# A pair-product kernel with batch normalisation: another order on GpSimd, and another cutting of the stores

## Chip, cores, metric

The kernel runs on one core of a Trainium2 chip. The metric is device time in microseconds. The profile is of one execution, and its span is about 1.7 us shorter than the timed figure of the same execution.

## The reference, cut

```python
# r_xi, r_xj: (1024, 39, 16); W: (1, 16, 16); gamma, beta: (741,)
rows, cols = np.tril_indices(39, k=-1)                   # 741 pairs (row, col), col < row
cross = xj[:, rows, :, None] * xi[:, cols, None, :]      # (1024, 741, 16, 16)
mean, var = ...                                          # of each pair, over (0, 2, 3)
normed = (cross - mean) * rsqrt(var + 1e-5) * gamma + beta
out = normed[:, :, None] * W                             # (1024, 1, 741, 16, 16), float32
```

The output has 777 MB, the inputs 6 MB. Row r has r pairs, "columns" below; one column of one sample is 256 floats in each of 128 partitions, 128 KB.

## The kernel before

Each partition holds 8 samples, worked on two at a time. A tile is one row for two samples. Row r and row 38-r share one half of a large buffer `y_sb`, and the two halves alternate. "Set" means such a pair of rows: 38 columns, two samples, 9.96 MB. The statistics, some 45 us at the start, are left out here.

```python
def products(n):                       # y = xj * (scaled xi): ScalarE 24 instructions a tile, GpSimd 8
    xs = xs_of.pop(n)
    for t in range(T):                 # T = 2 samples, sample 0 first
        for i in range(E):
            product(n, nc.scalar if i < E - POOL_I else nc.gpsimd, t, i, xs[:, t])

def store(n, c0, c1):
    r, t0, _ = tiles[n]
    n0 = first[r]
    nc.sync.dma_start(
        out_v[:, t0 : t0 + T, (n0 + c0) * EE : (n0 + c1) * EE],
        view(n)[:, :, c0:c1, :].rearrange("p t n e -> p t (n e)"),
    )

def bounds(r):                         # PIECE = 14
    pieces = -(-r // PIECE)
    return tuple(q * r // pieces for q in range(pieces + 1))

def finish(n):                         # y = (y + t) * w
    ...                                # GpSimd: the last 13% of the columns
    for c0, c1 in zip(bounds(r), bounds(r)[1:]):
        for c in range(c0, min(c1, split)):
            stt(...)                   # VectorE: one instruction a column, both samples
        store(n, c0, c1)

for n in range(1, len(tiles)):
    if n + 1 < len(tiles):
        products(n + 1)
    if n + 2 < len(tiles):
        scale_xi(n + 2)                # GpSimd
    if n >= RAW:                       # RAW = 2
        finish(n)
```

## Time and profile before

| | before |
|---|---|
| timed, median of 3 | 1929.05 us |
| span of the profiled run | 1927.5 us |
| VectorE, ScalarE, GpSimd busy | 90%, 86%, 79% |
| stores of the output | 289 |

No engine is busy for the whole span. The row to read is that of the transfers, stage by stage; the prediction shows it. A share of 1.01 is the highest that this profile holds over a whole stretch; it is read here as DMA engines that are never idle, and a lower share as engines that had to wait for pieces.

### The profile page before, as it was taken

What the parts mean: (1) busy time and instruction counts of PE and PEld (TensorE: products, weight loads), DVE (VectorE), ACT (ScalarE), POOL (GpSimd) and SP (SyncE); (2) the same over time, 40 slices, a digit from 0 to 9 for tenths busy, and PEclk for the clock granted to TensorE, in tenths of its full rate; (3) what the DMA queues carried; (4) which work ended last, traced back from release to release, by engine and by line L of the source; (5) the groups of instructions that cost most, each with busy time, mean ns of one, the idle gap of its engine ahead of it and who ended that gap; (6) DMA issues with size and microseconds to landing.
All of it is one profiled execution on the core that took longest, in us unless ns stands there. A gap on an engine that the chain in (4) does not pass through costs nothing. (4 is left out here: it accounts for less than half of the span.)

```text
span 1927.5 us, 10086 instructions
## 1 busy us (share of the span) xinstructions
PE 25.5 (1%) x132; PEld 23.8 (1%) x132; DVE 1732.3 (90%) x2603; ACT 1663.4 (86%) x3690; POOL 1528.2 (79%) x1918
## 2 busy tenths in 40 slices
PE   2200000000000000000000000000000000000000
PEld 2200000000000000000000000000000000000000
DVE  5999999999989899999999999999999999888886
ACT  7999888888888988889888898888888888888752
POOL 6898888887878787979787878888888877777654
DMA  3799999999999999999999999999999999999998
GB/s 125 326 421 421 420 421 421 421 421 421 424 426 423 424 425 423 426 423 426 423 421 421 421 421 416 411 420 416 414 415 414 415 414 415 405 406 402 393 389 373
DMA packets 80174, 783.66 MB, mean 407 GB/s; under 512 B 4800, under 2 KB 5824, under 8 KB 14816
## 3 DMA queue, kind: packets, MB, share of 16 engines
q1 hardware_dynamic: 79328, 779.95, 96.8%
q10 hardware_dynamic: 720, 2.94, 0.4%
q14 instruction: 77, 0.63, 0.1%
q0 software_dynamic: 48, 0.13, 0.1%
q8 instruction: 1, 0.02, 0.0%
HBM read 6.00 MB, written 776.99 MB: 406 GB/s over the span
## 5 line engine op out<-in xcount | busy, mean ns | idle before, releaser
L222 DVE SCALAR_TENSOR_TENSOR y_sb<-y_sb,st_sb,w_dve 128x512 f32<-128x512 f32 x2542 | 1679.7, 742 | 158.5 <-issue 147.1
L130 ACT ACTIVATE y_sb<-xs,xj_sb 128x256 f32<-128x256 f32 (+33 forms) x3600 | 1613.4, 542 | 218.7 <-DMA out_dram<-y_sb 166.2
L132 POOL TENSOR_SCALAR y_sb<-xs,xj_sb 128x256 f32<-128x256 f32 (+33 forms) x1200 | 604.3, 527 | 198.5 <-DMA out_dram<-y_sb 131.3
L214 POOL TENSOR_TENSOR y_sb<-y_sb,w_sb 128x1024 f32<-128x1024 f32 (+4 forms) x138 | 441.8, 3202 | 11.5
L150 POOL TENSOR_TENSOR xs<-xi_sb,st_sb 128x576 f32<-128x576 f32 (+37 forms) x150 | 188.0, 1253 | 146.4 <-ACT y_sb L130 146.4
L210 POOL TENSOR_SCALAR y_sb<-y_sb,st_sb 128x512 f32<-128x512 f32 x384 | 259.6, 693 | 1.7 <-ACT y_sb L130 1.7
L130 ACT ACTIVATE y_sb<-xi_sb,xj_sb 128x304 f32<-128x304 f32 x52 | 23.9, 533 | 0.0
L191 DVE TENSOR_TENSOR y_sb<-y_sb,w_dve 128x5120 f32<-128x5120 f32 (+3 forms) x5 | 20.9, 4205 | 3.2 <-ACT y_sb L181 3.2
L183 POOL TENSOR_SCALAR y_sb<-y_sb,st_sb 128x512 f32<-128x512 f32 x18 | 13.5, 772 | 7.5 <-DVE st_sb L396 7.5
L383 PE MATMUL ps<-y_sb 39*128 39x38 f32 (+37 forms) x76 | 16.9, 398 | 20.1 <-DVE st_sb L390 13.9
L383 PEld LDWEIGHTS ps<-y_sb 39*128 39x128 f32 x76 | 16.4, 328 | 20.7 <-DVE st_sb L390 14.2
L281 DVE TENSOR_REDUCE y_sb<-y_sb 128x78 f32<-128x1248 f32 x8 | 11.6, 1448 | 3.8 <-ACT y_sb L275 3.6
L266 POOL TENSOR_TENSOR y_sb<-xj_sb,y_sb 128x1248 f32<-128x1248 f32 x4 | 9.3, 2321 | 6.3 <-ACT y_sb L319 6.3
L181 ACT ACTIVATE y_sb<-y_sb,st_sb 128x512 f32<-128x512 f32 x20 | 14.2, 798 | 0.0
L260 DVE TENSOR_REDUCE y_sb<-xj_sb 128x78 f32<-128x1248 f32 x4 | 5.8, 1449 | 8.5 <-DMA xj_sb<-in_r_xj_dram 8.5
L275 ACT ACTIVATE y_sb<-y_sb 128x1248 f32<-128x1248 f32 x8 | 9.8, 1228 | 2.2 <-POOL y_sb L266 2.2
L266 POOL TENSOR_TENSOR y_sb<-xi_sb,y_sb 128x1248 f32<-128x1248 f32 x4 | 9.3, 2318 | 0.0
L130 ACT ACT_TABLE_LOAD x1 | 1.3, 1283 | 7.8 <-DMA xi_sb<-in_r_xi_dram 7.8
L298 PE MATMUL ps_g<-y_sb 128*39 128x79 f32 x48 | 7.2, 339 | 18.6 <-DVE y_sb L286 18.6
L298 PEld LDWEIGHTS ps_g<-y_sb 128*39 128x39 f32 x48 | 6.1, 183 | 19.5 <-POOL y_sb L266 11.2
L132 POOL TENSOR_SCALAR y_sb<-xi_sb,xj_sb 128x304 f32<-128x304 f32 x12 | 5.9, 509 | 0.0
L260 DVE TENSOR_REDUCE y_sb<-xi_sb 128x78 f32<-128x1248 f32 x4 | 5.8, 1442 | 0.0
(42 smaller groups left out, 23.3 us busy)
## 6 DMA issues: line engine op xcount, KB each, us to landing
out_dram<-y_sb SPq DMA_DIRECT2D x56, 3072.0 KB, 11.7
out_dram<-y_sb SPq DMA_DIRECT2D x56, 2816.0 KB, 13.7
out_dram<-y_sb SPq DMA_DIRECT2D x52, 2560.0 KB, 14.2
out_dram<-y_sb SPq DMA_DIRECT2D x32, 3328.0 KB, 16.5
out_dram<-y_sb SPq DMA_DIRECT2D x16, 3584.0 KB, 17.8
out_dram<-y_sb SPq DMA_DIRECT2D x23, 2304.0 KB, 15.6
out_dram<-y_sb SPq DMA_DIRECT2D x20, 2048.0 KB, 22.4
out_dram<-y_sb SPq DMA_DIRECT2D x8, 1792.0 KB, 18.9
```

Source lines behind the costliest of these rows:

```text
L130: nc.scalar.activation(y, src, AF.Copy, scale=scale)
L132: engine.tensor_scalar(y, src, scale, 1.0, ALU.mult, ALU.mult)
L150: nc.gpsimd.tensor_tensor(xs, xi_sb[:, t0 : t0 + T, 0:r, :], s_sb[:, :, n0 : n0 + r, :].to_broadcast([P, T, r, E]), ALU.mult,)
L181: nc.scalar.activation(y[:, :, c, :], y[:, :, c, :], AF.Identity, bias=t_c, scale=s_c)
L183: nc.gpsimd.tensor_scalar(y[:, :, c, :], y[:, :, c, :], s_c, t_c, ALU.mult, ALU.add)
L191: nc.vector.tensor_tensor(y[:, :, c0:c1, :], y[:, :, c0:c1, :], w_dve.unsqueeze(1).to_broadcast([P, T, c1 - c0, EE]), ALU.mult,)
L210: nc.gpsimd.tensor_scalar(y[:, :, c, :], y[:, :, c, :], t_sb[:, n0 + c : n0 + c + 1], 1.0, ALU.add, ALU.mult)
L214: nc.gpsimd.tensor_tensor(y[:, :, split:r, :], y[:, :, split:r, :], w_sb.unsqueeze(1).to_broadcast([P, T, r - split, EE]), ALU.mult,)
L222: stt(y[:, :, c, :], y[:, :, c, :], t_sb[:, n0 + c : n0 + c + 1], w_dve.to_broadcast([P, T, EE]), ALU.add, ALU.mult,)
L266: nc.gpsimd.tensor_tensor(devs[n % 7], sources[x][:, t0 : t0 + T], shift[:, x : x + 1, :].unsqueeze(3).to_broadcast([P, T, F, E]), ALU.sub ...
L298: nc.tensor.matmul(acc[0:F, 0 : 2 * F + 1], lhs, fb[:, t], start=t == 0, stop=t == NT - 1)
L383: nc.tensor.matmul(ps_v[:, :, first[r] - n0 : first[r] - n0 + r], pick[:, r, :], stq[:, :, 0:r], start=True, stop=True,)
```

## The change

The intent is to keep the transfers supplied in the late rows. GpSimd adds bias and weight to its own columns before it turns to products that may have to wait for a buffer. Rows over 28 leave in four pieces, the first and the last short, and the last piece in two stores, one for each sample. Rows up to 19 leave whole, except the first tile, whose three pieces stay.

```diff
-PIECE = 14
+WHOLE = 19
+LONG = 28
@@ def store
-        nc.sync.dma_start(
-            out_v[:, t0 : t0 + T, (n0 + c0) * EE : (n0 + c1) * EE],
-            view(n)[:, :, c0:c1, :].rearrange("p t n e -> p t (n e)"),
-        )
+        step = 1 if r > LONG and c1 == r else T
+        for t in range(0, T, step):
+            nc.sync.dma_start(
+                out_v[:, t0 + t : t0 + t + step, (n0 + c0) * EE : (n0 + c1) * EE],
+                view(n)[:, t : t + step, c0:c1, :].rearrange("p t n e -> p t (n e)"),
+            )
@@ def bounds
-        pieces = -(-r // PIECE)
-        return tuple(q * r // pieces for q in range(pieces + 1))
+        if r <= WHOLE:
+            return (0, r)
+        if r <= LONG:
+            return (0, r // 2, r)
+        return (0, r // 5, r // 2, r - r // 5, r)
@@ the loop over tiles
+            if n == 1:
+                products(2)
+                scale_xi(3)
+                continue
+            if n + 2 < len(tiles):
+                scale_xi(n + 2)
+            finish(n)
             if n + 1 < len(tiles):
                 products(n + 1)
-            if n + 2 < len(tiles):
-                scale_xi(n + 2)
-            if n >= RAW:
-                finish(n)
```

## The prediction

> **What bounds the kernel now.** I read the page first, its slices above all: they show which resource is full in which stage.
>
> ```profile
> span 1927.5 us, 10086 instructions
> DMA  3799999999999999999999999999999999999998
> GB/s 125 326 421 421 420 421 421 421 421 421 424 426 423 424 425 423 426 423 426 423 421 421 421 421 416 411 420 416 414 415 414 415 414 415 405 406 402 393 389 373
> ```
>
> From the third slice on, the transfers are full, with three levels of rate: 421, then about 424, then 421 again, and a decline from slice 25. No engine is full in the same sense: VectorE 90%, ScalarE 86%, GpSimd 79%. The table by stretch (columns: time, busy time and count of PE, PEld, DVE, ACT and POOL, granted clock, DMA share, GB/s) says what the levels are:
>
> ```profile
> 335.00:382.00 47.00, 0.00 (x0) 0.00 (x0) 42.68 (x65) 42.36 (x96) 38.95 (x50) 1.00 1.01 421
> ...
> 711.00:758.00 47.00, 0.00 (x0) 0.00 (x0) 42.27 (x65) 41.43 (x94) 34.41 (x47) 1.00 1.01 424
> ...
> 1087.00:1134.00 47.00, 0.00 (x0) 0.00 (x0) 43.63 (x66) 41.72 (x96) 38.79 (x50) 1.00 1.01 422
> ...
> 1557.00:1604.00 47.00, 0.00 (x0) 0.00 (x0) 42.27 (x65) 41.76 (x96) 37.11 (x47) 1.00 0.99 414
> ...
> 1792.00:1839.00 47.00, 0.00 (x0) 0.00 (x0) 40.79 (x63) 34.61 (x54) 33.07 (x29) 1.00 0.94 394
> 1839.00:1886.00 47.00, 0.00 (x0) 0.00 (x0) 41.80 (x65) 27.31 (x40) 27.57 (x29) 1.00 0.91 383
> ```
>
> A "set" below is row r with row 38-r for two samples: always 38 columns, 38 x 256 KB = 9.96 MB. With rows 20 to 23 a set leaves in four transfers (two pieces of each row) at 421.1 GB/s, with rows 24 to 28 in three (the short row is whole) at 424.3, with rows 29 and 30 in four (the long row in three pieces) at 421 again, each time with the share at 1.01. So one more transfer per set costs 9.96/421.1 - 9.96/424.3 = 0.18 us, and the bytes alone take 23.48 - 3 x 0.18 = 22.94 us (434 GB/s). Below a share of 1.01 the transfers starve. Why they do at the end is in the chain of work that ended last (start, us, what):
>
> ```profile
> 1833.23 5.62 POOL y_sb L214
> ...
> 1838.86 9.46 DMA out_dram<-y_sb
> ...
> 1848.60 6.00 POOL y_sb L132 x8
> 1854.60 2.23 POOL xs L150
> 1856.83 3.35 POOL y_sb L210 x5
> ...
> 1860.24 5.60 POOL y_sb L214
> ...
> 1865.86 9.46 DMA out_dram<-y_sb
> ```
>
> This is a ring: the last piece of a tile leaves (9.46), which frees the buffer for GpSimd's products (6.00); behind these in GpSimd's order stand the scaling of xi (2.23) and the finishing of the previous tile's own pairs (3.35 + 5.60), which releases that tile's last piece. It comes to 27.0 us per set of row 38, where three transfers need 23.5. Last, the beginning, in the two-us stretches:
>
> ```profile
> 76.00:78.00 2.00, 0.00 (x0) 0.00 (x0) 2.00 (x4) 2.00 (x6) 2.00 (x5) 1.00 0.99 415
> 78.00:80.00 2.00, 0.00 (x0) 0.00 (x0) 2.00 (x4) 2.00 (x6) 2.00 (x3) 1.00 0.05 19
> 80.00:82.00 2.00, 0.00 (x0) 0.00 (x0) 2.00 (x4) 2.00 (x6) 1.92 (x3) 1.00 0.00 0
> 82.00:84.00 2.00, 0.00 (x0) 0.00 (x0) 2.00 (x4) 2.00 (x6) 2.00 (x3) 1.00 0.61 253
> ```
>
> Here the queue is empty and waits for the third tile's first piece, while VectorE is full. It stays full until about 240: in that time the backlog of transfers is only building up.
>
> **What the Trainium skill says.** "SBUF — State Buffer", section "The DMA setup-cost knee", puts the asymptote at 16 ports x 27.2 GB/s = 436 GB/s; the 434 GB/s found above from the two levels agrees, so the saturated middle has nothing left but the cost of cutting. "DMA: Bandwidth & Descriptors", section "Measured (HBM→SBUF, 128 partitions, SWDGE, issued from GpSimd)", gives about 10.5 ns per packet in tiny loads. Each store here has 256 rows, 16 per DMA engine, and one completion packet: 17 x 10.5 = 0.179 us, close to my 0.18. This trace cannot say whether the price is per packet or per transfer, since all its stores have the same number of rows; the change has stores of 128 rows, and there it matters. The same page, "Rules for kernel authors", wants at least 1 MiB per DMA; the new half pieces of 5 to 7 columns have 0.66 to 0.92 MB, so the direction of that cost is against the change. "GPSIMD Engine Reference", section 3.1, puts a two-input operation near 2.5 cycles an element; the trace's 5.60 us for 2560 elements are 2.19 ns, 2.6 cycles at the page's 1.2 GHz. It agrees, and the finishing cannot be had for less: it can only be moved.
>
> **The change, part by part.**
> 1. *GpSimd finishes first.* The same instructions, in another order. It takes the ring apart: the finishing of tile n no longer stands behind products that wait for a transfer. What remains for row 38 is a ring over two sets: last piece landed, ScalarE's 24 products 16.7 us (24 instructions in 16.73), VectorE's 33 instructions 21.8 us (33 in 21.81), last piece. GpSimd has 2.2 + 9.0 after ScalarE's last product, inside VectorE's 21.8, and so drops out.
> 2. *Rows over 28 in four pieces.* For row 38: 7, 12, 12, 7 columns instead of 12, 13, 13. VectorE does only 2 of the last 7 (GpSimd has five), and the transfer that frees sample 0 is 7 x 128 KB: 2.1 us, plus 1.7 us to land (9.46 for 3.4 MB, less 7.8 at 434 GB/s; an estimate). The ring: 16.7 + 21.8 + 2.1 + 1.7 = 42.3 us for two sets, plus whatever backlog stands ahead of it; two sets of transfers take 47 to 48. So the transfers should be full again in rows 31 to 38, with 5 us to spare in the worst row and more in the others.
> 3. *Its price.* Rows 29 to 38 go from three transfers to five: 40 tiles x 2 = +80. Rows 15 to 19 whole: 16 tiles less one each, and three of the four tiles of row 19: -19. From 289 to 350, +61. Per transfer: 61 x 0.18 = +11.0 us. Per packet: 310 x 16 + 350 data and completion packets per engine instead of 289 x 17, +397 x 10.6 ns = +4.2 us. A full set of rows 29 to 37 would then run at 9.96/(22.94 + 6 x 0.18) = 415 GB/s, or about 418 per packet. That is what rows 31 to 35 have now, starved: there the change wins nothing or little; rows 29 and 30 lose.
> 4. *Row 19 whole.* The third tile's first piece now leaves after 9 VectorE instructions (0.66 us each), the whole tile after 17. The queue is empty then, so it stays empty 8 x 0.66 = 5.3 us longer, and as everything behind it is full, this shifts all. The second tile whole leaves 5 us later too, but both its halves are out before 88 either way. I add nothing for rows 15 to 18.
>
> The sum. Before: first bytes at 50.2; transfers 78 sets x 22.94 + 289 x 0.18 = 1841.3; idle from 50 to 84, from the shares of the stretches, 8.8; end of the last bytes to end of span 2.0 (stretches of the end). Left over: 1927.5 - 1902.3 = 25.2 us of starving, nearly all after 1180 (the rates of the 47-us stretches from 1181 against 421 give 20 up to 1886, and the tail the rest). After: 50.2 + 1789.3 + (56 to 63 of cutting, middle 60) + 8.8 + 5.3 + 2.0 + remaining starving. For that last term I take 5 us: 0.5 us a set in row 38, where the ring with its backlog is nearly as long as two sets, somewhat less in 36 and 37, and a residue. Sum 1920.6 us of span; the timed figure stands 1.5 over the span, so **1922 us**, a gain of 0.4%. In short: +20 from the ring, -8 from cutting, -5 from the start.
>
> **Rivals.**
> - *The price is per transfer.* Then 1925; per packet, 1919. For packets speaks the 17 x 10.5; for transfers, that each has its own completion. The rates of rows 29 to 37 will tell: 415 or 418.
> - *GpSimd becomes the late one elsewhere.* Its products of n+1 now come after the finishing of n, so VectorE could wait at the start of n+1 for GpSimd instead of ScalarE. Then the transfers would starve in the middle, and with the price of cutting the time would be about 1940 to 1945. Against it: in row 38 GpSimd needs 2.2 + 9.0 + 6.0 = 17 us after ScalarE's last product, and VectorE is busy on tile n for 21.8 of them; with rows 27 and 11, GpSimd's 12 us stand beside 15 us of VectorE. The order gives GpSimd no work more.
> - *The early backlog is too thin for whole rows.* Until 240 VectorE is full at 21.8 us a set against 23.5 of transfer. By hand: whole row 19 leaves at 87 and runs to 99, the next leaves at 98; row 20's pieces at 105 and 110 and whole row 18 at 120 meet a queue busy to 111, 117 and 123. It holds, with half a us to spare at one place; if not, 3 to 8 us more: 1925 to 1930.
> - *Much faster.* Even with all starving and all cutting gone, 50.2 + 1789.3 + 14.1 + 2.0 = 1856 would be the end; with the cutting that this profile prices, 1912 to 1919. A gain of 2% (1890.5) is out of reach unless cutting is free.
>
> **Range and chances.** Low end 1911: price per packet and no starving left make 1913.5, two less for what I round. High end 1936: price per transfer, half the starving stays and the start costs more. All of it lies within 2% (1890.5 to 1967.6). Faster 0.01, same 0.97, slower 0.02 (a new wait in the middle that I don't see).
>
> **What would show it.** Step 1: no GpSimd products or finishing in the chain at the end, and the DMA share after 1650 back at 1.00 to 1.01. Step 3: 415 to 418 GB/s in rows 29 to 37 at full share (now 421 in rows 29 and 30), 424 in rows 20 to 23 (now 421). Step 4: the queue empty from 83 to 88 instead of 78 to 83. Wrong would be: VectorE waiting for GpSimd's products in the middle, a share under 1.00 between 90 and 1180, or rows 29 and 30 still at 421, which would make cutting cheaper than I think.

## The result

The changed kernel takes 1924.28 us (median of 6, 1924.05 to 1924.9) against 1929.10 for the kernel before on the same chip: ratio 0.9976, interval 0.9963 to 0.9989. That is a gain of 0.24%, which at a threshold of 2% is "same".

The slices of the profile after:

```profile
span 1923.2 us, 10490 instructions
...
DMA  3699999999999999999999999999999999999999
GB/s 125 273 425 423 425 425 424 424 425 425 424 425 423 424 425 426 423 424 424 423 418 419 417 418 418 418 417 416 411 412 413 415 412 412 412 410 412 412 412 391
```

The decline at the end has nearly gone, but from row 29 on the level before it is lower. The same stretches as were shown of before:

```profile
335.00:382.00 47.00, 0.00 (x0) 0.00 (x0) 41.43 (x64) 39.99 (x91) 36.40 (x51) 1.00 1.01 425
1087.00:1134.00 47.00, 0.00 (x0) 0.00 (x0) 42.56 (x66) 41.33 (x95) 39.15 (x50) 1.00 1.01 418
1557.00:1604.00 47.00, 0.00 (x0) 0.00 (x0) 42.44 (x65) 42.35 (x96) 37.42 (x49) 1.00 1.00 413
1792.00:1839.00 47.00, 0.00 (x0) 0.00 (x0) 42.30 (x65) 36.76 (x65) 37.47 (x39) 1.00 0.99 409
1839.00:1886.00 47.00, 0.00 (x0) 0.00 (x0) 43.63 (x66) 31.03 (x46) 32.17 (x29) 1.00 0.99 412
```

Against before: rows 20 to 23 gain (421 to 425 in the first line), rows 29 and 30 lose at a full share (422 to 418 in the second), row 35 is about the same (414 and 413), and the last rows gain (394 and 383 to 409 and 412). The chain of work at the end:

```profile
1837.27 9.70 DMA out_dram<-y_sb
...
1847.08 2.14 ACT y_sb L132 x3
...
1849.87 4.48 ACT y_sb L132 x7
1854.35 6.59 DVE y_sb L230 x10
...
1860.99 10.63 DMA out_dram<-y_sb
```

GpSimd has left the chain. In its place is transfer, ScalarE's products, VectorE, transfer. The beginning, in two-us stretches:

```profile
66.00:68.00 2.00, 2.00 (x10) 2.00 (x10) 2.00 (x1) 2.00 (x6) 0.00 (x0) 1.00 0.07 31
68.00:70.00 2.00, 0.13 (x1) 0.00 (x1) 2.00 (x1) 2.00 (x6) 0.00 (x0) 1.00 0.00 0
70.00:72.00 2.00, 0.67 (x3) 0.67 (x4) 1.97 (x3) 0.71 (x2) 0.80 (x1) 1.00 0.36 150
...
82.00:84.00 2.00, 0.00 (x0) 0.00 (x0) 2.00 (x4) 2.00 (x6) 0.00 (x0) 1.00 0.46 195
84.00:86.00 2.00, 0.00 (x0) 0.00 (x0) 2.00 (x4) 2.00 (x6) 1.81 (x2) 1.00 0.00 0
86.00:88.00 2.00, 0.00 (x0) 0.00 (x0) 2.00 (x4) 2.00 (x5) 1.92 (x3) 1.00 0.00 0
88.00:90.00 2.00, 0.00 (x0) 0.00 (x0) 2.00 (x4) 2.00 (x6) 2.00 (x3) 1.00 0.75 315
```

The queue is empty from 83 to 88.5, where before it was empty from 78 to 83. That stretch is about as long as before, only later. The additional 5 us of idle time lie at 66 to 71, before the second tile, which is whole too; the kernel before has shares of 0.89 to 1.06 there.

### The profile page after: what moved, and what is told of

Read it like the earlier page. It is cut to its first block, busy times and chain, and to the rows that moved or that the text cites. A ratio compares the mean times of both kernels' runs of the same rounds, so it can differ in the third digit from the quotient of the medians.

```text
span 1923.2 us, 10490 instructions
## 1 busy us (share of the span) xinstructions
PE 25.5 (1%) x132; PEld 23.8 (1%) x132; DVE 1733.6 (90%) x2602; ACT 1663.9 (87%) x3690; POOL 1534.1 (80%) x1918
## 5 line engine op out<-in xcount | busy, mean ns | idle before, releaser
L196 DVE TENSOR_TENSOR y_sb<-y_sb,w_dve 128x1536 f32<-128x1536 f32 (+3 forms) x4 | 20.9, 5219 | 3.2 <-ACT y_sb L186 3.2
L391 PE MATMUL ps<-y_sb 39*128 39x38 f32 (+37 forms) x76 | 16.9, 398 | 20.1 <-DVE st_sb L398 13.9
L391 PEld LDWEIGHTS ps<-y_sb 39*128 39x128 f32 x76 | 16.4, 328 | 20.7 <-DVE st_sb L398 14.2
L289 DVE TENSOR_REDUCE y_sb<-y_sb 128x78 f32<-128x1248 f32 x8 | 11.6, 1448 | 3.5 <-ACT y_sb L283 3.3
L186 ACT ACTIVATE y_sb<-y_sb,st_sb 128x512 f32<-128x512 f32 x20 | 14.2, 800 | 0.0
L306 PEld LDWEIGHTS ps_g<-y_sb 128*39 128x39 f32 x48 | 6.1, 183 | 19.5 <-POOL y_sb L274 11.2
```

Of the source, the lines that this page charges most:

```text
L186: nc.scalar.activation(y[:, :, c, :], y[:, :, c, :], AF.Identity, bias=t_c, scale=s_c)
L196: nc.vector.tensor_tensor(y[:, :, c0:c1, :], y[:, :, c0:c1, :], w_dve.unsqueeze(1).to_broadcast([P, T, c1 - c0, EE]), ALU.mult,)
L306: nc.tensor.matmul(acc[0:F, 0 : 2 * F + 1], lhs, fb[:, t], start=t == 0, stop=t == NT - 1)
L391: nc.tensor.matmul(ps_v[:, :, first[r] - n0 : first[r] - n0 + r], pick[:, r, :], stq[:, :, 0:r], start=True, stop=True,)
```

## The experiments

All were correct, and all were timed over five rounds (four or five runs of each) beside the kernel before, whose median was between 1929.2 and 1929.6 us. Four calls were made: the first four runs, the next three, the four after those, and the last. Runs of one call shared a chip. The theory at the start is the prediction's: GpSimd's order breaks the ring that starves the late rows, and the cutting and the whole row 19 mostly cost. The rival is that the pieces break it and the order does nothing.

### 1. The order alone

```diff
 (kernel before, the loop over tiles alone)
-            if n + 1 < len(tiles):
-                products(n + 1)
+            if n == 1:
+                products(2); scale_xi(3)
+                continue
             if n + 2 < len(tiles):
                 scale_xi(n + 2)
-            if n >= RAW:
-                finish(n)
+            finish(n)
+            if n + 1 < len(tiles):
+                products(n + 1)
```

> The kernel before with only GpSimd's order changed (289 stores as before). Theory 1 (the order breaks the ring, the cutting and the whole row 19 only cost): no starving ring is left, so 50.2 + 1841.3 of transfers + 8.8 idle at the start + 2.0 + 5 to 8 of starving (the last piece of 13 columns makes the two-set ring 16.7 + 21.8 + 7.8 + 1.7 = 48.0 us against 47, so rows 36 to 38 stay a little short) = 1907 to 1910 of span, 1909 to 1912 us timed, that is 12 to 15 us under the whole change. Rival (the short last pieces break the ring, the order does nothing): 1929 us as before, with GpSimd's products and finishing still in the chain at the end.

It took 1927.15 us (ratio 0.9989, 0.9975 to 1.0002). The theory falls: 12 to 15 us less than the whole change were expected, and it was 3 us more. GpSimd did leave the chain, as it should, and the time hardly moved. The timeline of ScalarE in row 38 shows why (start, duration, what, idle before it and what ended that):

```profile
1821.73 16.73 ACT L130 ACTIVATE y_sb<-xs,xj_sb 128x608 f32<-128x608 f32 x24 [7.26 <-DMA out_dram<-y_sb]
1849.37 16.72 ACT L130 ACTIVATE y_sb<-xs,xj_sb 128x608 f32<-128x608 f32 x24 [10.91 <-DMA out_dram<-y_sb]
1872.66 16.73 ACT L130 ACTIVATE y_sb<-xs,xj_sb 128x608 f32<-128x608 f32 x24 [6.58 <-DMA out_dram<-y_sb]
```

From the first start to the third are two sets: 50.9 us, or 25.5 for each. In the kernel before the same three starts are at 1821.50, 1848.50 and 1875.42, 27.0 for each. So a second ring, ScalarE to VectorE to the last piece, was nearly as long as the GpSimd ring. The chain of this run has the last piece landing 11.6 to 12.8 us after its issue in this stage, not 9.5. The likely reason is the piece before it, still in the queue: it has 13 columns, 7.8 us of transfer at 434 GB/s, and was issued 8 VectorE instructions (5.3 us) earlier. An estimate: the 2.5 us left, 7.8 of its own and 1.7 to land make 12.0.

### 2. The pieces alone

```diff
 (whole change, that edit of the loop undone)
-            finish(n)
             if n + 1 < len(tiles):
                 products(n + 1)
+            if n + 2 < len(tiles):
+                scale_xi(n + 2)
+            if n >= RAW:
+                finish(n)
```

> The whole change, but GpSimd's old order. Theory 1: the ring stays, shorter by its last piece: products 6.0 + scaling 2.2 + finishing 9.0 + last piece 4.2 and 1.7 to land = 23.1 us and whatever stands ahead of it in the queue, against 23.8 of transfers in row 38; with the cost of cutting (+4) and the start (+5) between 1928 and 1938 us. Rival (the pieces alone break the ring): 1924 us, like the whole change.

It took 1925.03 us (ratio 0.9977), beside 0.9976 for the whole change. In time the rival holds: within the whole change the order adds nothing that can be measured. GpSimd did not leave this chain, though. It stands in it from 1847 to 1887, with 24.6 us between its starts (1847.03 and 1871.66), and the ScalarE ring has 24.7 (1822.15 to 1871.58 for two sets). With the new pieces the two rings are equally long, so taking one away gains nothing.

### 3. Without the halves

```diff
-        step = 1 if r > LONG and c1 == r else T
+        step = T
```

> The whole change, but the last piece of the long rows in one store instead of one for each sample (310 stores instead of 350, the same data packets). If cutting costs by packet: 40 completion packets less, -0.4 us, and at most +4 from the ring, which is 2.1 us longer: 1924 to 1928 us, with rows 29 and 30 still at 418 GB/s. If cutting costs by transfer: -7.2 us, 1917 to 1920 us, rows 29 and 30 at 421.

It took 1932.50 us (ratio 1.0016, 1.0003 to 1.0028), outside both expectations: 40 stores fewer, and 8 us slower. Rows 29 and 30 stayed at 417 to 418 GB/s, which speaks against a price by transfer. But the halves are worth far more than I gave them. Without them the last pieces land 11.9 to 12.8 us after their issue in the chain, where the whole change has 9.7 to 10.6, and the rate of the last rows (1792 to 1886) is 391 GB/s at a share of 0.94, where the whole change has 410 at 0.99.

### 4. Row 19 in two pieces again

```diff
-        if r <= WHOLE:
+        if r == WHOLE:
+            return (0, r // 2, r)
+        if r <= WHOLE:
             return (0, r)
```

> The whole change, but row 19 still in two pieces (three more stores). Theory: the queue's empty stretch at the third tile ends at 83 again instead of 88, and as everything behind it is full the whole 5.3 us come back, less 3 x 0.18: 1919 to 1920 us. Rival (the early shift is swallowed later by the wait of the last rows): 1924 us.

It took 1923.04 us (ratio 0.9965): 1.2 us under the whole change, not 5, and its own runs spread over 1.5 us. A gap opened later, at a share below 1.01 with VectorE nearly full (stretch of this run):

```profile
100.00:194.00 94.00, 0.00 (x0) 0.00 (x0) 93.25 (x143) 87.14 (x199) 80.39 (x101) 1.00 0.99 415
```

### 5 and 6. What cutting costs, where the transfers are full

```diff
 (5: kernel before, each store of rows 20 to 28 cut by samples)
+        step = 1 if 20 <= r <= 28 else T
+        for t in range(0, T, step): ...
 (6: kernel before, rows 20 to 28 in four pieces of columns)
-        pieces = -(-r // PIECE)
+        pieces = 4 if 20 <= r <= 28 else -(-r // PIECE)
```

> The kernel before, with each store of rows 20 to 28 (in the stretch where the transfers are full) cut by samples: 72 stores more, the same data packets, 72 completion packets more on each DMA engine. By packet: 72 x 10.6 ns = +0.8 us, 1930 us, the rate of rows 24 to 28 still about 424 GB/s. By transfer: 72 x 0.18 = +13 us, 1942 us, 9.96/(22.94 + 5 x 0.18) = 418 GB/s there.

> The kernel before, with rows 20 to 28 cut into four pieces of columns instead of two: 72 stores more, as in the run with halves, but also 72 x 16 data packets more on each engine. By packet: 72 x 17 x 10.6 ns = +13 us. By transfer: the same +13 us. So about 1942 us in both, rows 24 to 28 at 418 GB/s; only the pair with the run with halves tells them apart. A result near 1929 here would mean that cutting is free and the levels of rate have another cause.

Both have 72 stores more than the kernel before. By samples: 1930.39 us (ratio 1.0005, 0.9992 to 1.0019), 1.15 us over the median before. By columns: 1943.18 us (ratio 1.0071, 1.0059 to 1.0084), 13.9 us over. A stretch that is nearly all row 26, of the run by samples and then of the run by columns:

```profile
664.00:758.00 94.00, 0.00 (x0) 0.00 (x0) 86.43 (x133) 84.43 (x192) 77.54 (x101) 1.00 1.01 425
```

```profile
664.00:758.00 94.00, 0.00 (x0) 0.00 (x0) 84.73 (x129) 83.19 (x189) 76.00 (x98) 1.00 1.01 418
```

The kernel before has 425 in that stretch. A packet here is what the profile counts as one: each row of a store, and one completion packet for each store on each of the 16 engines. The store queue has 79328 packets in the kernel before, 72 x 16 more in run 5 and 72 x 16 x 17 more in run 6. So the same number of additional transfers costs about 1 us or 14 us, according to whether they bring additional data packets. The price is by packet: 13.9 us over 72 x 17 packets on each DMA engine is 11.4 ns, close to the 10.6 ns that the levels of rate had given (0.18 us over 17).

### 7. The order, with rows 15 to 18 whole

```diff
 (run 1, and)
-        pieces = -(-r // PIECE)
+        pieces = 1 if r < 19 else -(-r // PIECE)
```

> The kernel before with GpSimd's new order, rows 15 to 18 whole, row 19 and the long rows cut as before (273 stores): the parts that should help without those that should cost. Against the run of the order alone 16 x 0.18 = -2.9 us: 1906 to 1909 us. If the backlog between 90 and 240 is too thin for whole rows of 18: no gain on the order alone.

It took 1926.06 us (ratio 0.9983, beside 0.9989 for the order alone). The figure missed because it was built on run 1's expectation, which had already fallen. The difference, about 1 us instead of 2.9, has the same cause as in run 4: this run too has 415 GB/s from 100 to 194 and then 424 to 425 where the order alone has 421.

### 8. Rows 18 and 19 in two pieces

```diff
 (whole change, and)
+        if r in (18, 19):
+            return (0, r // 2, r)
```

> The whole change, but rows 18 and 19 still in two pieces each (seven stores more, all at the start, where VectorE sets the pace). With row 19 alone cut only 1.2 us came back of 5.3, and that run had a new gap between 100 and 194 (415 GB/s at a share of 0.99). If whole row 18 was that gap: 5.3 - 7 x 0.18 = -4.0 us, 1920 us, and no stretch under a share of 1.01 from 90 to 1180. If the loss lies elsewhere: 1923 us, as with row 19 alone.

It took 1920.72 us (ratio 0.9957), as expected, and the early gap is closed:

```profile
100.00:194.00 94.00, 0.00 (x0) 0.00 (x0) 94.00 (x144) 91.64 (x209) 87.08 (x113) 1.00 1.01 421
```

So whole rows cost at the start, where VectorE sets the pace and the queue has no backlog, row 18 as well as row 19. Cutting row 19 alone mostly moved the wait to row 18; cutting row 18 alone was not tried.

### 9. Four pieces in rows 36 to 38 only

```diff
 (run 8, and)
+        if r <= 35:
+            return (0, r // 3, r * 2 // 3, r)     # as before, and no halves here
```

> As the run with rows 18 and 19 cut, but rows 29 to 35 in three plain pieces as before; only rows 36 to 38 in four with halves. Theory (a packet costs 10.6 ns, and the starving that the four pieces cure sits in rows 36 to 38): rows 29 and 30 back at 421 GB/s (-1.6 us), rows 31 to 35 at 415 instead of 412.5 (-2.9 us): 1915 to 1917 us. If the short pieces matter in rows 31 to 35 too: 1920 to 1925 us, with the rate there under 412.

It took 1916.28 us (ratio 0.9932), as expected: rows 29 and 30 are at 421 GB/s again, and rows 31 to 35 at 414 to 418.

### 10 and 11. Halves without short pieces

```diff
 (11: kernel before with its old order; in store, the loop over samples with)
+        step = 1 if r > 28 and c1 == r else T
 (10: the same, with the new order and rows to 17 whole)
+        pieces = 1 if r < 18 else -(-r // PIECE)
```

> The kernel before with one thing changed: the last piece of rows 29 to 38 leaves by samples (40 stores more, no data packet more). If the halves are the cure: both rings get shorter by up to 3.9 us (half of the last piece's 7.8), 1915 to 1921 us. If they work only together with GpSimd's new order or with short pieces: 1926 to 1930 us.

> The kernel before with GpSimd's new order, rows to 17 whole, everything else cut as before, but the last piece of rows 29 to 38 leaving by samples, which adds completion packets only. If the halves were what cures the last rows (without them the whole change was 8 us slower), the ring of row 38 is 16.7 + 21.8 + 3.9 + 1.7 + 1 to 2 of backlog = 45 to 46 us for two sets that need 47: 50.2 + 1789.3 + 277 x 0.18 + 8.8 + 2.0 + 13 of starving = 1913 of span, 1913 to 1917 us. If the short first and last pieces are needed: 1922 to 1926 us.

Run 11, which differs from the kernel before only in that the last piece of the long rows leaves in two stores, took 1913.67 us (ratio 0.9919, 0.9905 to 0.9932). That is 15.9 us under the kernel before and more than three times the gain of the whole change. Run 10 took 1910.42 us (ratio 0.9903, 0.9888 to 0.9918). Both came out lower than expected. GpSimd's timeline of run 11 in row 38 shows what the halves do:

```profile
1835.44 3.01 POOL L132 TENSOR_SCALAR y_sb<-xs,xj_sb 128x608 f32<-128x608 f32 x4 [5.62 <-DMA out_dram<-y_sb]
1839.36 3.02 POOL L132 TENSOR_SCALAR y_sb<-xs,xj_sb 128x608 f32<-128x608 f32 x4 [0.91 <-DMA out_dram<-y_sb]
1842.34 2.26 POOL L150 TENSOR_TENSOR xs<-xi_sb,st_sb 128x1216 f32<-128x1216 f32 x1
```

The first half lands about 4 us before the second. GpSimd's four products of sample 0 are done by the time sample 1 is free, and 3.0 us have left the GpSimd ring. It goes from 27.0 us a set to 24.35 (the next such start is at 1859.79), since the issue of the second store, 0.34 us in the chain, comes in. ScalarE starts at 1835.36 as well, and needs sample 1 only after twelve products. In run 10, with the new order, three ScalarE starts of row 38 are at 1809.08, 1833.25 and 1856.61: 47.5 us for two sets, where run 1 had 50.9. Runs 8 and 10 differ in one thing, the columns of rows 29 to 38 in four pieces or in three, and were timed together: 1920.72 and 1910.42. The four pieces cost 10.3 us. The packets are 40 x 17 x 10.6 ns = 7.2 us of it by the price above. For the rest, the rates from 1510 to 1886 (412, 413, 410, 412 against 414, 417, 416, 416) show that the four pieces don't supply the queue any better. The first half of row 38's last piece, first of 7 columns (run 8) and then of 13 (run 10), from issue to landing:

```profile
1856.74 10.67 DMA out_dram<-y_sb
```

```profile
1847.80 8.71 DMA out_dram<-y_sb
```

The shorter half lands later. VectorE has only 2 of the last 7 columns, so the last piece is issued 1.3 us after a piece of 12 columns (7.2 us at 434 GB/s) and stands behind it. An estimate from these numbers: 5.9 us ahead, 2.1 of its own and 1.7 to land make 9.7; with pieces of 13 columns 2.5 + 3.9 + 1.7 = 8.1. Between runs 11 and 10 the order adds little again: of the 3.3 us, the 12 stores fewer (rows 15 to 17) are 12 x 17 x 10.6 ns = 2.2.

### 12. Rows 29 to 32 in two pieces

```diff
 (run 10, and)
-        pieces = 1 if r < 18 else -(-r // PIECE)
+        pieces = 1 if r < 18 else 2 if r <= 32 else 3
```

> As the combined run (1910.4 us), but rows 29 to 32 in two pieces instead of three, the last still by samples. Theory (a packet costs 10.6 ns, the half that frees a sample is what the ring sees): the half is 15 to 16 columns of one sample, 2.1 MB, 4.8 us, no longer than the 13 columns of both before; 16 x 0.18 = -2.9 us, 1907 to 1909 us, rows 29 to 32 at 424 GB/s. If pieces of 16 columns starve the queue, because VectorE works 10 us on one: 1911 to 1918 us.

It took 1909.22 us (1907.68 to 1909.28; ratio 0.9896, 0.9879 to 0.9912). It is the fastest by its median, about 1% under the kernel before. Against run 10, timed in another call, the difference is inside the intervals. The rate from 946 to 1228 is 423 to 424 GB/s, where run 10 has 421, at a share of 1.00 to 1.01.

## Why the prediction was right, and where it was not

The time was forecast at 1922 us and measured at 1924.3, inside the range, and "same" was right. Two errors in the sum cancelled in part. That the time came out so close was partly luck: the change held the halves, which do most of the curing, beside the order, which got the credit. The same working, applied to the order alone, gave 1909 to 1912 us, and run 1 took 1927.15.

**The bound.** Right. The transfers set the time in the saturated middle, and 22.94 us for a set plus a price for cutting fits the middle of the runs (425 GB/s and 418 in runs 5 and 6).

**Step 3, the price of cutting.** Left open between 4 and 11 us, and by packet it is 4. In rows 29 and 30 the change ran at 417 to 418 GB/s, as the price by packet said, and runs 5 and 6 settled it directly. The 17 x 10.5 ns that spoke for it was weaker than it looked: the page's figure is 0.67 us of a whole 4 KB load over its 64 packets, and the page does not say how many of them ran on each engine. I entered the middle, 60 us of cutting; by packet it is 5310 x 10.6 ns = 56.

**Step 4, row 19 whole.** Right in its size: from 50 to 88 the shares of the changed kernel give 14.2 us of idle, against 8.8 + 5.3 in the sum. But the additional idle time lies before the second tile, and it does not end at 88: stretches of two us at 92, 100 and 108 have shares of 0.80, 0.73 and 0.73, where the kernel before has none under 0.96, so the rival of the thin early backlog came true by about 1 us (the shares from 88 to 194 give 1.0 us of idle time, against 0.2 before). "I add nothing for rows 15 to 18" hid something too: row 18 whole makes a gap of its own once row 19 doesn't (runs 4 and 8).

**The term mis-sized: the starving that remains.** I put it at 5 us, most of it in row 38. With 56 for cutting and 14.2 at the start, the span of 1923.2 leaves 1923.2 - 50.2 - 1789.3 - 56.3 - 14.2 - 2.0 = 11.2 us. Rows 32 to 38 all run at 408 to 417 GB/s and shares of 0.99 to 1.01, not at 418. The sentence that failed is "the ring: 16.7 + 21.8 + 2.1 + 1.7 = 42.3 us for two sets, plus whatever backlog stands ahead of it" with "5 us to spare": the backlog was named and then counted as nothing. The ring in the changed kernel (ScalarE, VectorE, and ScalarE's next start in the same half of the buffer):

```profile
1822.30 16.73 ACT L132 ACTIVATE y_sb<-xs,xj_sb 128x608 f32<-128x608 f32 x24 [7.00 <-DVE y_sb L230]
...
1839.12 21.81 DVE L230 SCALAR_TENSOR_TENSOR y_sb<-y_sb,st_sb,w_dve 128x512 f32<-128x512 f32 x33 [1.91 <-issue]
...
1871.73 16.73 ACT L132 ACTIVATE y_sb<-xs,xj_sb 128x608 f32<-128x608 f32 x24 [7.92 <-DMA out_dram<-y_sb]
```

The two ScalarE starts are 49.4 us apart for two sets that need 47 to 48. The products and VectorE took what the prediction said; the first half of the last piece took 10.63 us to land (at 1860.99 in the chain above), not 2.1 + 1.7 = 3.8. Row 38's ring explains 1.4 to 2.4 us for each two sets; what holds rows 32 to 37 under 418 is not shown.

**Steps 1 and 2, what cures the late rows.** Here the mechanism was wrong in its weights. The prediction gave the credit to GpSimd's order, with the short pieces beside it, and mentioned the halves for 2 us in one ring. The runs show the order worth about 2 us alone (an interval that reaches no gain) and nothing measurable within the change. The short pieces, first and last together, are worth less than nothing (10 us of loss, run 8 against 10), and the halves carry it (8 us of gain within the change, 16 alone). The GpSimd ring was real in the chain, but a second ring of 25.5 us a set stood right behind its 27.0. The halves shorten both: ScalarE starts when sample 0 is released, and GpSimd has that sample's products done before sample 1 is. "Much faster" was ruled out at 2%, and nothing tried here reached it.

What stays open: why rows 34 to 38 still run at 414 to 417 GB/s instead of 421 in the best runs. The shares of 0.99 to 1.00 say that short waits remain, and I have not found which.

## What to carry to other kernels

When a buffer is freed by its last store, look at who needs which part of it first, and let that part land in a store of its own: cutting along a dimension whose rows are separate packets anyway brings completion packets only, and 72 such cuts cost about 1 us here. Cutting a contiguous row shorter was paid by packet while the queue was full, 14 us for 72 cuts. A short last piece lands no sooner when a long one was issued just before it. And before taking one ring off the chain of waits, work out the length of the next, with the queue ahead of its transfer counted: the chain shows only the longest.

## What the Trainium skill lacked or had wrong

- "DMA: Bandwidth & Descriptors", section "Measured (HBM→SBUF, 128 partitions, SWDGE, issued from GpSimd)", gives about 10.5 ns per packet, for tiny loads, without saying whether that is per DMA engine. The runs show 11.4 ns (runs 5 and 6) and 10.6 ns (from the levels of rate) for a packet on each of the 16 engines, in full store queues with data packets of some 5 to 14 KB. The agreement may be chance. The page does not work out what cutting a large transfer costs.
- The same page's "Rules for kernel authors" (at least 1 MiB per DMA, coalesce) and the summary of "SBUF — State Buffer" (one DMA, not several) don't say that a transfer's completion can be the bound. Two stores in place of one for the last piece of 40 tiles, for the same bytes, made the kernel 15.9 us faster (run 11), and 72 more stores in a full queue cost about 1 us (run 5).
- "SBUF — State Buffer", section "Summary: rules for kernel authors", says to estimate transfers between HBM and SBUF at about 358 GB/s. With one core running, the stores here went at 421 to 425 GB/s for over 800 us, near the 436 GB/s that the same page gives for the SBUF ports. The summary lacks the condition: "DMA: Bandwidth & Descriptors", in the section named first, has 425 GB/s for loads of 16 MB with the other core of the pair idle.
